# SyncE's and GpSimd's instructions in program order, with several loads moved, in a spectral-convolution and dilation kernel

## The chip, the core and the metric

The kernel runs on one core of a Trainium2 chip. TensorE (PE) multiplies matrices, VectorE (DVE) and ScalarE (ACT) work on tiles, GpSimd (POOL) and SyncE (SP) here do little but issue transfers (DMAs) between the main memory and the on-chip memory. Each engine works through its own instructions in order; engines wait for each other and for transfers through semaphores. The metric is the device time of one execution in microseconds (us). The kernel before takes 4047.03 us, the median of 3 runs (4043.34 to 4052.0).

## The reference

The input x has 8 images of 8 channels in 4 groups, 256 x 256 pixels each, in float32.

```python
def ref(x, ...):                           # cut to what matters
    # layer 0: x + FNO(groupnorm(x))
    h = gconv1x1(concat(x_normed, gridx, gridy), fc0)     # 2 + 2 -> 10 channels in each of 4 groups
    for i in range(4):
        h1 = irfft2(12 x 12 low modes of rfft2(h), lo and hi, times sp_w1[i], sp_w2[i])
        h2 = gconv1x1(h, w_w[i], w_b[i])
        h = h1 + h2
        if i < 3:
            h = x*sigmoid(x*softplus(beta))/1.1 of h
    h = the same swish of gconv1x1(h, fc1)                # 10 -> 128 channels per group
    x = x + gconv1x1(h, fc2)                              # 128 -> 2 channels per group
    # layer 1: x + 3x3 dilation (max over the window, border -2) of groupnorm(x)
    return x + dilate3x3(groupnorm(x))
```

## The kernel before

Each image goes through four spectral layers, in which its state h stays on the chip in 11 chunks of 128 x 2048 numbers; the last layer stores the chunks to main memory. The "head" (fc1, swish, fc2: 128 steps) of an image reads them back in pieces hs and runs interleaved with the four layers of the next image. The dilation of the image before that runs in between. Beside the last layer of an image, the spectrum of the next image's x is made (`start`). The Python code records the instructions; inside `manual_schedule` the engines listed keep the order of the code. In this kernel these are TensorE, VectorE and ScalarE; the order of SyncE and GpSimd is chosen by the scheduler.

```python
    def load_x(b):                                   # 2 transfers of 1 MB
        src = a["x"][b].rearrange("c (p i f) -> (c p) i f", p=16, i=2)
        for i in range(2):
            nc.sync.dma_start(turned[:, i], src[:, i])
    ...
    def spectrum_x(b, out_):
        x = turned[:, 0:2]
        if b > 0:
            load_x(b)
        yield 1.5 * SIDE
        ...                                          # batch-norm statistics, transposes, transforms
    def load_sw(l, k):                               # 400 KB of spectral weights, two buffers "sw"
        t = sb.tile([128, G, 2 * WID, WID], F32, tag="sw")
        nc.sync.dma_start(t.rearrange("p g m i -> p (g m i)"), a["spw"][l, k])
        return t

    def mix(b, l, out_):
        ...
        for k in range(3):
            for k2 in range(2):
                pr = turned[:, 2, 1024 * k2 : 1024 * k2 + 800].rearrange(...)
                nc.vector.tensor_tensor(pr, sw[k], bt[:, k2, k]..., ALU.mult)          # L360
                yield 0.7
                nc.vector.tensor_reduce(s[k2][:, k]..., pr..., AX.X, ALU.add)          # L363
                if k == 0 and k2 == 1:
                    sw.append(load_sw(l, 2))
                yield 0.7
        ...
        nc.vector.tensor_tensor(f[:, 0], ..., ALU.subtract)                            # L371
        nc.vector.tensor_tensor(f[:, 1], ..., ALU.add)
        ...                                          # p_f: matmuls of fold with f        L379
    def layer(b, l, out_, stored, side):
        ...
        def burst(c):
            pair = [ps_z(f"p_z_{b}_{l}_{c}_{i}") for i in range(2)]
            ...                                      # L477 (l = 0) or L480, then L483, into pair
            for i in range(2):
                dst = h[:, c, 2 * i : 2 * i + 2, :]
                if l < 3:
                    nc.scalar.activation(dst, pair[i], AF.Silu)                        # L489
                else:
                    nc.scalar.activation(dst, pair[i], AF.Identity, bias=bias3)        # L491
            if l == 3:
                nc.sync.dma_start(stored[c], h[:, c].rearrange("p f w -> p (f w)"))    # L493, 1 MB

        def read_x(c):                               # 4 transfers of 48 KB
            for g in range(G):
                nc.sync.dma_start(
                    h[32 * g : 32 * g + 6, c].rearrange("p f w -> p (f w)"), a["xp"][b, c, g])
        if l == 0:
            for c in range(NCH):
                read_x(c)
            ...
        if l == 3:
            room = 0.0
            yield "odd"
            for c in range(NCH):
                burst(c)
                room += SIDE
                while room > 0.0:
                    room -= next(side, SIDE)         # side: start() of the next image
                yield (LAST,)                        # two head steps
            return
        ...
    def start(b, out_):
        if b < n_img:
            out_["sw"] = [load_sw(0, 0), load_sw(0, 1)]
            yield from spectrum_x(b, out_)
            for n in mix(b, 0, out_):
                yield 1.4 * n
    ...
    def head(b, stored, stats):
        ...
        def load_state(k):                           # 256 KB, four buffers "hs"
            if k < NQ * NCH:
                j, c = k // NCH, k % NCH
                hs[k] = sb.tile([128, PIX], F32, tag="hs", bufs=4, name=f"hs_{b}_{k}")
                nc.sync.dma_start(hs[k], stored[c][:, PIX * j : PIX * (j + 1)])
        def first(n):
            ...                                      # 8 matmuls L628, 2 activations L630
        def second(n):
            ...                                      # at n % 16 == 0 also the load of y; matmuls L650
            ...                                      # add to y on VectorE, L653 or L655
        load_state(0)
        load_state(1)
        for n in range(STEPS):
            if n % 32 % NBLK == 0:
                load_state(n // 32 * NCH + n % 32 // NBLK + 2)
            if n % 2 == 0 and n > 3:
                second(n - 4)
            first(n)
            yield
        second(STEPS - 4)
        second(STEPS - 2)
```

Line numbers such as L360 are those of the kernel before.

## Time and profile before

| engine | busy us | share of 4041.6 us |
|---|---|---|
| TensorE matmuls | 3734.7 | 92% |
| ScalarE | 2853.1 | 71% |
| VectorE | 2538.8 | 63% |
| GpSimd | 117.0 | 3% |

The transfers move 345.05 MB, 85 GB/s on average. The profiled execution took 4041.6 us. The views show, in this order: the busy share of each engine, in 40 equal slices a digit for tenths of the slice (9 is 90% or more); groups of instructions as "line engine operation, what it writes <- what it reads, count | busy us, mean ns | idle us before them and what ended it"; waits as "engine line <- who ended it: total us, times, longest us"; and the timeline as "start us, duration us, engine, line, operation". SPq is SyncE's queue: its entries are the issuing of a transfer, not the transfer. PEld is the loading of weights into TensorE.

### The profile page before, as it was taken

What the parts mean: (1) busy time and instruction counts of PE and PEld (TensorE: products, weight loads), DVE (VectorE), ACT (ScalarE), POOL (GpSimd) and SP (SyncE); (2) the same over time, 40 slices, a digit from 0 to 9 for tenths busy, and PEclk for the clock granted to TensorE, in tenths of its full rate; (3) what the DMA queues carried; (4) which work ended last, traced back from release to release, by engine and by line L of the source; (5) the groups of instructions that cost most, each with busy time, mean ns of one, the idle gap of its engine ahead of it and who ended that gap; (6) DMA issues with size and microseconds to landing.
All of it is one profiled execution on the core that took longest, in us unless ns stands there. A gap on an engine that the chain in (4) does not pass through costs nothing.

```text
span 4041.6 us, 118640 instructions
## 1 busy us (share of the span) xinstructions
PE 3734.7 (92%) x53530; PEld 1463.3 (36%) x53530; DVE 2538.8 (63%) x3535; ACT 2853.1 (71%) x2991; POOL 117.0 (3%) x202
## 2 busy tenths in 40 slices
PE   5666999999999999999999999999999999999997
PEld 2333333433333333333433333333333333333221
DVE  6765656556766666766666666666676666673533
ACT  3334777777777777777777777777777777778886
POOL 1000000000000000000000000000000000000000
PEclk8888999999999999999999999999999999999998
DMA  3005111432125321252122611144121532215311
GB/s 85 14 14 188 53 33 41 139 123 58 58 67 166 93 59 58 82 189 56 55 64 89 197 44 53 53 134 151 55 59 51 164 109 63 61 48 194 96 53 46
DMA packets 113985, 345.05 MB, mean 85 GB/s; under 512 B 15768, under 2 KB 18392, under 8 KB 98056
## 3 DMA queue, kind: packets, MB, share of 16 engines
q1 hardware_dynamic: 95288, 276.33, 22.0%
q0 software_dynamic: 18192, 61.13, 4.7%
q8 instruction: 422, 6.91, 0.7%
q14 instruction: 83, 0.68, 0.1%
HBM read 213.40 MB, written 123.74 MB: 83 GB/s over the span
## 4 chain that ended last, share of the span: by engine, by line
PE 78%; DVE 11%; ACT 7%; issue 3%; DMA 1%; POOL 0%; DVEq 0%; POOLq 0%; SPq 0%; ACTq 0%
PE p_fc L650 22%; PE p_fc L628 20%; PE p_z L483 8%; PE p_z L480 7%; PE p_d L448 6%; ACT act L630 4%; PE p_u L462 3%; PE p_z L477 3%; DVE turned L431 2%; PE p_b L333 2%; PE p_g L405 2%; PE p_g L410 2%; ACT h L491 2%; DVE turned L324 2%; DVE turned L201 1%
## 5 line engine op out<-in xcount | busy, mean ns | idle before, releaser
L630 ACT ACTIVATE act<-p_fc 128x1024 f32<-128x1024 f32 x2048 | 1960.1, 1026 | 669.6 <-PE p_fc L628 665.3
L628 PE MATMUL p_fc<-hs,c_w 32*128 32x512 f32 x8192 | 1204.4, 631 | 14.8 <-DVE turned L195 8.5
L650 PE MATMUL p_fc<-act,c_w 128*32 128x512 f32 x8192 | 997.5, 601 | 47.1 <-ACT act L630 35.5
L628 PEld LDWEIGHTS p_fc<-hs,c_w 32*128 32x128 f32 x8192 | 402.3, 183 | 697.3 <-ACT act L630 278.5
L489 ACT ACTIVATE h<-p_z 128x1024 f32<-128x1024 f32 x528 | 511.7, 1021 | 190.5 <-PE p_z L483 189.8
L431 DVE STREAM_TRANSPOSE turned<-h 128x1024 f32<-128x1024 f32 x528 | 623.2, 1219 | 23.4 <-ACT h L489 23.1
L655 DVE TENSOR_TENSOR y<-p_fc,y 128x512 f32<-128x512 f32 x392 | 270.6, 690 | 497.1 <-PE p_fc L650 496.1
L650 PEld LDWEIGHTS p_fc<-act,c_w 128*32 128x32 f32 x8192 | 227.5, 109 | 645.6 <-issue 345.5
L483 PE MATMUL p_z<-c_binv,zt 32*128 32x256 f32 x5632 | 411.7, 405 | 0.6 <-ACT zt L193 0.6
L480 PE MATMUL p_z<-h,c_wt 32*32 32x512 f32 x8448 | 371.1, 601 | 6.7 <-DVE y L655 3.4
L483 PEld LDWEIGHTS p_z<-c_binv,zt 32*128 32x128 f32 x5632 | 261.6, 186 | 305.4 <-issue 295.8
L448 PE MATMUL p_d<-turned,c_fw 32*32 32x480 f32 (+1 forms) x9216 | 309.9, 540 | 11.1 <-DVE turned L431 11.1
L195 DVE COPY zt<-p_g 128x264 f32<-128x264 f32 x300 | 162.6, 629 | 167.1 <-PE p_g L410 91.6
L491 ACT ACTIVATE h<-p_z,c_bias 128x1024 f32<-128x1024 f32 x176 | 186.5, 1111 | 38.8 <-PE p_z L483 38.4
L199 ACT ACTIVATE turned<-p_d 128x960 f32<-128x960 f32 x144 | 130.1, 903 | 94.5 <-PE p_d L448 94.5
L363 DVE TENSOR_REDUCE S<-turned 128x80 f32<-128x800 f32 x192 | 188.8, 983 | 4.7
L448 PEld LDWEIGHTS p_d<-turned,c_fw 32*32 32x32 f32 x9216 | 121.5, 103 | 187.1 <-issue 150.6
L360 DVE TENSOR_TENSOR turned<-t,B 128x800 f32<-128x800 f32 x192 | 188.6, 982 | 0.9 <-DMA t<-in_spw 0.8
L462 PE MATMUL p_u<-turned,c_stack 128*32 128x480 f32 (+1 forms) x1152 | 137.3, 546 | 42.9 <-DVE turned L201 42.9
L324 DVE STREAM_TRANSPOSE turned<-zt 128x960 f32<-128x960 f32 x96 | 175.6, 1857 | 0.6
L201 DVE COPY turned<-p_d 128x960 f32<-128x960 f32 x144 | 152.1, 1057 | 28.9 <-PE p_d L448 28.7
L480 PEld LDWEIGHTS p_z<-h,c_wt 32*32 32x32 f32 x8448 | 93.7, 103 | 211.2 <-ACT act L630 69.1
(169 smaller groups left out, 1964.8 us busy)
## 6 DMA issues: line engine op xcount, KB each, us to landing
stored<-h SPq DMA_DIRECT2D x88, 1024.0 KB
hs<-stored SPq DMA_DIRECT2D x352, 256.0 KB
t<-in_spw SPq DMA_DIRECT2D x96, 400.0 KB
yin<-y_rows POOLq DMA_DIRECT2D x56, 512.0 KB, 5.0
h<-in_xp SPq DMA_DIRECT2D x352, 48.0 KB
turned<-in_x SPq DMA_DIRECT2D x16, 1024.0 KB
y<-in_x SPq DMA_DIRECT2D x56, 256.0 KB
y_rows<-y POOLq DMA_DIRECT2D x56, 256.0 KB, 2.3
```

Source lines behind the costliest of these rows:

```text
L324: nc.vector.transpose(rows[:, 960 * g : 960 * (g + 1)].rearrange("p (i r) -> p i r", r=32), windows(g))
L431: nc.vector.transpose(dst[:, 2 * i : 2 * i + 2], h[:, c, 2 * i : 2 * i + 2].rearrange("p f (s x) -> p f s x", s=2))
L448: mm(pair[q // 2][part(v % 4), q % 2, : 240 * n], fw8[part(q), v, :], t[part(q), :, :, v, : NBLK * WID], start=v < 4, stop=v >= 4)
L462: mm(p[part(g), : 240 * n], stack, m, start=True, stop=True)
L480: mm(o, wt[part(q), l, g, :], h[part(q), c, f, :], start=True, stop=False)
L483: mm(pair[q // 2][:, q % 2, HW * s : HW * (s + 1)], zt[part(q), 2 * c + s].rearrange("p f o -> p (f o)"), binv[part(q), :], start=False, s ...
L489: nc.scalar.activation(dst, pair[i], AF.Silu)
L491: nc.scalar.activation(dst, pair[i], AF.Identity, bias=bias3)
L628: mm(pair[g // 2][:, g % 2, :], w1[part(g), blk, :], hs[k][part(g), :], start=True, stop=True)
L630: nc.scalar.activation(act[:, 2 * i : 2 * i + 2, :], pair[i], AF.Silu)
L650: mm(acc[part(g), :], w2[:, g, 15 - rb - i : 47 - rb - i], act[:, g, :], start=i == 0, stop=i == 1)
L655: nc.vector.tensor_tensor(y, sums, y, ALU.add)
```

## The change

SyncE and GpSimd join the engines that keep the order of the code. Since the scheduler then no longer moves loads ahead, the code asks for some of them in other places: the next image's x in front of the last layer, the first layer's x at first for four chunks and then four chunks ahead of each burst, the first two pieces of the head's state in the last burst of the last layer, and each y of the head eight steps before the first use. The arithmetic and the instructions of TensorE, VectorE and ScalarE are unchanged.

```diff
+AHEAD = 4
...
     def spectrum_x(b, out_):
         x = turned[:, 0:2]
-        if b > 0:
-            load_x(b)
         yield 1.5 * SIDE
...
+    def read_x(b, c):
+        for g in range(G):
+            nc.sync.dma_start(
+                h[32 * g : 32 * g + 6, c].rearrange("p f w -> p (f w)"), a["xp"][b, c, g])
...
         def burst(c):
+            if l == 0 and c + AHEAD < NCH:
+                read_x(b, c + AHEAD)
+            if l == 3 and c == NCH - 1:
+                for k in range(2):
+                    out_["pieces"][1](k)
             pair = [ps_z(f"p_z_{b}_{l}_{c}_{i}") for i in range(2)]
...
         if l == 0:
-            for c in range(NCH):
-                read_x(c)
...
                 yield from mix(b, l, d)
+            if l == 3 and b + 1 < n_img:
+                load_x(b + 1)
+            if l == 0:
+                for c in range(AHEAD):
+                    read_x(b, c)
             yield from rows_of(b, l)
...
-    def head(b, stored, stats):
-        hs, acts, box = {}, {}, {}
+    def pieces_of(b, stored):
+        hs = {}
+        def load_state(k):
+            if k < NQ * NCH and k not in hs:
+                ...                                  # as before
+        return hs, load_state
+
+    def head(b, pieces, stats):
+        hs, load_state = pieces
+        acts, ys = {}, {}
...
+        def load_y(t):
+            ...
+            nc.sync.dma_start(y, a["x"][b]...[:, t])
...
-        load_state(0)
-        load_state(1)
+        load_y(0)
         for n in range(STEPS):
+            if n % 16 == 8 and n // 16 < 7:
+                load_y(n // 16 + 1)
...
-    with tc.manual_schedule(engines={PE, DVE, ACT}):
+    with tc.manual_schedule(engines={E.PE, E.DVE, E.Activation, E.SP, E.Pool}):
...
+            d["pieces"] = pieces_of(b, stored)
```

## The prediction

> **What bounds the kernel now.** I read the page's busy shares and 40 slices first, then the busy time by stretch of one image, then the waits of each engine, and last the timelines of SyncE, VectorE (DVE), ScalarE (ACT) and TensorE (PE) around the end of an image's last layer.

> Span, TensorE and its slices, from the page:

> ```profile
> span 4041.6 us, 118640 instructions
> PE 3734.7 (92%) x53530; PEld 1463.3 (36%) x53530; DVE 2538.8 (63%) x3535; ACT 2853.1 (71%) x2991; POOL 117.0 (3%) x202
> ...
> PE   5666999999999999999999999999999999999997
> ```

> TensorE is full except in the first four slices (image 0 alone, no head beside it) and the last (the last head alone). Two steady images, busy time by engine (PE, PEld, DVE, ACT, POOL, clock, DMA share, GB/s):

> ```profile
> 900.00:1380.00 480.00, 462.72 (x6670) 180.29 (x6656) 318.18 (x442) 352.69 (x368) 14.68 (x24) 1.00 0.29 91
> 1380.00:1860.00 480.00, 462.69 (x6658) 179.64 (x6650) 318.75 (x443) 350.60 (x366) 14.69 (x24) 0.99 0.29 91
> ```

> An image gives TensorE 17.3 us of idleness in 480, and the DMA engines are busy for only 0.29. TensorE's largest waits from 420 to 3760 us:

> ```profile
> PE p_u L462 <- DVE turned L201: 35.5, 45, 2.4
> PE p_fc L650 <- ACT act L630: 21.6, 75, 0.5
> PE p_fc L650 <- ACT h L491: 10.6, 47, 0.3
> PE p_b L333 <- DVE turned L324: 9.9, 14, 0.7
> ```

> No transfer is among them. On VectorE, transfers end 33 us of idleness in the whole run: the dilation's reads (22.2 and 4.6), two small loads at the start (3.6 and 2.0) and one spectral weight:

> ```profile
> L360 DVE TENSOR_TENSOR turned<-t,B 128x800 f32<-128x800 f32 x192 | 188.6, 982 | 0.9 <-DMA t<-in_spw 0.8
> ```

> So there is no wait for a transfer to win back in the steady part. I compared the instructions of the two programs: those of TensorE, VectorE and ScalarE stand in the same sequence; only SyncE's and GpSimd's queues differ. The question is therefore only whether something lands later than it is needed.

> [...] a 0.4 MB weight issued 0.4 us after a 1 MB store was usable 5.5 us later. [...] the page of this kernel shows one hardware queue, with 276 of the 345 MB. [...] the trace has them, 116 before the first layer's matmuls with a median of 51 ns.

> **The change, part by part.**

> (1) *Next image's x ahead of the last layer.* The before queue already had it there: it was issued at 726.44 us, and the batch-norm statistics that read it started at 771.27. Now it follows the mix of layer 3, some 741 to 745 us on that clock. Two MB, at the 338 to 416 GB/s that the busiest 5 us stretches of the trace show, take 6 us; it lands 18 us early at least. Effect: 0.

> (2) *First layer's x four chunks ahead.* The first 16 of 44 small reads now follow the last store; the rest come one chunk per burst. Before, 30 of them took 22.15 us from 372.18, or 0.74 us each. Sixteen take 12 us. In the first steady boundary the last store is issued at 848.09, so they would be out by 860; layer 0's first matmul is at 868.17 and needs only the first four. Each later chunk has four bursts' lead, above 20 us. Effect: 0.

> (3) *Head's loads.* hs_0 and hs_1 now go just before the last store (about 841 us), the first head matmul that needs them is at 860.43: 19 us for 256 KB. y_0 and hs_2 follow the 16 reads at about 861; the add that needs y_0 comes after 871, hs_2 is used from step 6, after 885. Later hs loads wait for a buffer freed about ten steps before use; a step is 480/128 = 3.75 us. In the last head y_0 waits for the edge fills, now after the store of y at 3739.77, so about 3741; it is needed at 3749.40. Effect: 0.

> (4) *Program order on SyncE.* Here is the loss. The third weight of the next image's first mix (t, k = 2) is asked for when the first product frees a buffer. Before, the scheduler let it pass ahead of store 9. In program order it stands behind store 9, which waits for ScalarE's copy of burst 9; hs_0 follows it. At all seven boundaries the new queue reads store 9, t, hs_0. SyncE before, at the first steady boundary:

> ```profile
> 831.91 0.35 SPq L350 DMA_DIRECT2D t<-in_spw  x1
> ...
> 833.51 0.35 SPq L493 DMA_DIRECT2D stored<-h  x1
> ...
> 841.27 0.35 SPq L493 DMA_DIRECT2D stored<-h  x1
> ```

> The copy that frees store 9, the products of k = 2 that need t, the sum after them, and TensorE's next step, each from its engine's timeline:

> ```profile
> 837.76 2.12 ACT L491 ACTIVATE h<-p_z,c_bias 128x1024 f32<-128x1024 f32 x2 [0.20 <-PE p_z L483]
> ...
> 841.53 0.98 DVE L360 TENSOR_TENSOR turned<-t,B 128x800 f32<-128x800 f32 x1
> ...
> 847.32 0.69 DVE L655 TENSOR_TENSOR y<-p_fc,y 128x512 f32<-128x512 f32 x1 [1.86 <-PE p_fc L650]
> 847.92 0.27 DVE L371 TENSOR_TENSOR F<-S,S 128x120 f32<-128x120 f32 x1
> ...
> 848.34 1.02 PE L379 MATMUL p_f<-F,c_fold 32*32 32x120 f32 x32
> ```

> How long t takes behind a store is seen at image 0's boundary, on SyncE and then VectorE:

> ```profile
> 367.15 0.35 SPq L493 DMA_DIRECT2D stored<-h  x1
> 367.59 0.38 SPq L350 DMA_DIRECT2D t<-in_spw  x1
> ...
> 373.12 0.99 DVE L360 TENSOR_TENSOR turned<-t,B 128x800 f32<-128x800 f32 x1 [0.83 <-DMA t<-in_spw]
> ```

> That is 373.1 - 367.15 = 5.95 us after the store's issue. Now the sum for the first steady boundary: the copy ends at 837.76 + 2.12 = 839.9, store 9 goes at 840.0 and t is usable at about 846.0 instead of being there at 841.5: VectorE stands 4.4 us. Its two products and two reductions take 4 x 0.98, to 849.9; the add of y pushes the sum F to 0.6 later, 850.5, and L379 starts 0.4 after F, at 850.9 in place of 848.34: 2.6 us. The difference to 4.4 is the 1.86 us that VectorE stood idle there already. The same working gives 2.5 us at the second boundary (copy ends about 1321.5, need 1323.39, L379 at 1329.96) and 2.0 at the third (copy ends 1802.9, need 1805.33, L379 at 1811.91); the other three look like the third (copy ends 2288.15, need 2290.57, L379 at 2297.15). At image 0's boundary store 9 was issued at 369.58, so t would come at 375.5 instead of 373.1 with TensorE already waiting: 2.4 us. Sum: 2.4 + 2.6 + 2.5 + 4 x 2.0 = 15.5 us. TensorE is in order and full, so most of it stays; ScalarE catches up during the stall and saves perhaps a few of the later short waits, so I book 13.

> (5) *Waits.* The new program has 49 more EventSemaphores on TensorE, 11 more on VectorE and 67 fewer on ScalarE. At 51 ns they would be +2.5, +0.6 and -3.4 us were they all exposed; most are behind running work. Booked: -1.

> (6) *GpSimd in program order.* Before, the edge fills of the last head blocked GpSimd for 33.6 us at 3646 to 3680 us; that is gone, but TensorE had no wait for the dilation there. In steady images one read of yin moves behind two stores of y, which are done before the last layer begins; its reader comes one burst into that layer. Effect: 0.

> Prediction: 4047 + 13 - 1 = 4059 us, 0.3% slower.

> **Rivals.** *No difference, or a small gain.* If t lands in 3 us rather than 5.5, VectorE's 1.86 us of slack hides nearly all of it, and the lighter ScalarE queue decides: 4040 to 4050. For it speaks that the small x reads no longer share the queue in that stretch; against it that the store in front is the same. *A blocked SyncE queue starves the head.* One queue in program order means any store or buffer wait holds up all behind it. If hs or x came too late each burst of layers 0 and 3 would wait: 1 us on 22 bursts in 7 images is 154 us, 4200. Against it stands the lead of 10 us or more for each of them in (2) and (3). *A faster steady part.* That would need idleness ended by transfers; TensorE has 17.3 us per image in all, 7 x 17.3 = 121 us, and none of its waits names one.

> **Range and chances.** The delay per boundary may be 0 to 3.5 us, over seven boundaries 0 to 25; the effects booked at zero add some 5 us either way. From 4047 that gives 4042 to 4077, which I move down a little for the lighter ScalarE queue: 4040 to 4076. Two per cent is 81 us: a gain of that size would take two thirds of the steady idleness and can't come from transfers, chance 0.01; a loss needs the starved head, 0.03; within 2%, 0.96.

> **What would show it.** In the changed profile VectorE's product with t (L360's group) should have idleness ended by the DMA t<-in_spw of some 20 to 30 us, in seven waits of 2 to 4.5 us, where there was one of 0.8. TensorE should have waits of about 2 us more than before at p_f on VectorE's F, once per boundary, and its busy time in a steady image should stay at 463 us while the image takes 482 to 484. No wait of TensorE should name hs or in_xp. It is wrong if t shows no wait, if TensorE waits for a transfer, or if the stretch up to 330 us moves by more than 2 us.

## The result, and the profile after

The changed kernel took 4086.03 us (median of 4 executions, 4080.85 to 4087.45) beside 4045.59 us for the kernel before. The ratio is 1.0095, with a 95% interval of 1.0078 to 1.0113. A second series gave 4080.59 beside 4049.87, ratio 1.0086 (1.0058 to 1.0114). The prediction was 4059 with a range to 4076: the direction was right, the size was less than half of what came.

The page of the kernel after, span, busy time and slices:

```profile
span 4083.4 us, 118516 instructions
PE 3757.7 (92%) x53530; PEld 1470.7 (36%) x53530; DVE 2538.0 (62%) x3535; ACT 2853.3 (70%) x2991; POOL 117.1 (3%) x202
PE   5666999999999999999999999999999999999997
```

TensorE, VectorE, ScalarE and GpSimd execute as many instructions as before. VectorE and ScalarE are as busy as before to within a microsecond, but TensorE's busy time grew from 3734.7 to 3757.7 us with the same 53530 matmuls. So this is not only a matter of waiting: the same matmuls lasted longer.

The predicted part is there. The product with the third weight t, in the groups of the page:

```profile
L359 DVE TENSOR_TENSOR turned<-t,B 128x800 f32<-128x800 f32 x192 | 188.4, 981 | 23.9 <-DMA t<-in_spw 23.8
```

That is 23.8 us of idleness where there was 0.8. TensorE's largest waits from 420 to 3760 us:

```profile
PE p_u L466 <- DVE turned L202: 35.5, 45, 2.4
PE p_fc L662 <- ACT act L651: 20.7, 74, 0.3
PE p_f L378 <- DVE F L370: 11.2, 6, 2.3
PE p_fc L662 <- ACT h L500: 9.9, 45, 0.3
```

The third line is new: six waits of TensorE for F, up to 2.3 us. No wait of TensorE names hs or in_xp. The other lines stand much as before.

The first steady boundary, on SyncE, ScalarE, VectorE and TensorE, each from its engine's timeline (start, length, what it is, and in brackets the idleness before it):

```profile
851.47 0.32 SPq L502 DMA_DIRECT2D stored<-h  x1
851.88 0.39 SPq L349 DMA_DIRECT2D t<-in_spw  x1
...
849.32 2.12 ACT L500 ACTIVATE h<-p_z,c_bias 128x1024 f32<-128x1024 f32 x2 [0.20 <-PE p_z L492]
...
857.36 0.99 DVE L359 TENSOR_TENSOR turned<-t,B 128x800 f32<-128x800 f32 x1 [4.19 <-DMA t<-in_spw]
...
861.81 0.27 DVE L370 TENSOR_TENSOR F<-S,S 128x120 f32<-128x120 f32 x1
...
862.23 1.82 PE L378 MATMUL p_f<-F,c_fold 32*32 32x120 f32 x32 [2.30 <-DVE F L370]
```

ScalarE's copy ends at 851.44, store 9 goes at 851.47, t behind it, and t is usable at 857.36: 5.89 us after the store, where 5.95 was reckoned. VectorE stands 4.19 us (4.4 reckoned) and TensorE 2.30 us (2.6 reckoned).

Two things in these traces were in no step of the prediction. The first is in the last line: the 32 matmuls of p_f take 1.82 us, and took 1.02 before. The busy time by stretch around them (PE, PEld, DVE, ACT, POOL, then the granted TensorE clock, DMA share and GB/s):

```profile
855.20:862.00 6.80, 4.54 (x44) 1.42 (x36) 4.57 (x7) 6.20 (x7) 0.00 (x0) 1.00 0.82 299
862.00:865.40 3.40, 3.17 (x42) 2.03 (x42) 1.50 (x8) 0.00 (x0) 0.00 (x0) 0.51 0.41 82
865.40:872.00 6.60, 6.60 (x48) 2.54 (x40) 3.22 (x6) 4.76 (x5) 0.00 (x0) 1.00 0.43 93
...
892.70:903.00 10.30, 10.30 (x78) 3.07 (x70) 2.90 (x5) 5.71 (x6) 0.00 (x0) 0.50 0.25 58
```

For 3.4 us from the end of the wait, and again for 10.3 us from 892.7, TensorE runs at half its clock (0.51 and 0.50 granted) while it is busy for 3.17 of the 3.40 us and for all of the 10.30. Between 386 and 3740 us the clock records of this trace hold 64.8 us of such stretches, each 3.41 us long or a multiple; the trace of before holds 27.3 us. By estimate, half of the 37.5 us more is lost, about 18.8 us, if TensorE is busy throughout.

The second is in layer 0's second burst of each image. TensorE's timeline there, the kernel before and then the kernel after, with ScalarE's of the kernel after below it:

```profile
874.09 1.18 PE L477 MATMUL p_z<-h,wcn 6*32 6x512 f32 x32
```

```profile
889.41 1.05 PE L486 MATMUL p_z<-h,wcn 6*32 6x512 f32 x4
890.65 1.14 PE L486 MATMUL p_z<-h,wcn 6*32 6x512 f32 x28 [0.19 <-ACT act L651]
...
889.58 1.94 ACT L651 ACTIVATE act<-p_fc 128x1024 f32<-128x1024 f32 x2 [1.05 <-PE p_fc L649]
```

Before, the 32 matmuls start together. After, four start and the others come 1.24 us later, when ScalarE has read the first half of a head tile: 889.58 plus half of 1.94 is 890.55. Most of that wait counts as busy: the four that run cover 1.05 of the 1.24 us, and 0.19 are idle. The instructions are the same. What they wait for is not, as the two programs say of the second PSUM tile of this burst:

```
before  L477 Matmult p_z, layer 0, chunk 1, second half <- h,wcn   waits: DMA, VectorE
after   L486 Matmult p_z, layer 0, chunk 1, second half <- h,wcn   waits: DMA, ScalarE
```

All tiles in PSUM, the memory into which TensorE writes, share four buffers, and the scheduler chooses one for each tile. With SyncE and GpSimd in program order it has chosen otherwise: 28 of the 4001 tiles follow another tile in their buffer than before. One of them at each of the seven boundaries is this one, which now takes a buffer that ScalarE frees late, while a head tile gets the one that VectorE had freed. By what rule the scheduler chooses is not shown.

### The profile page after: what moved, and what is told of

It reads as the page before. It is cut to its first block, busy times and chain, and to the rows that moved or that the text cites. A ratio compares the mean times of both kernels' runs of the same rounds, so it can differ in the third digit from the quotient of the medians.

```text
span 4083.4 us, 118516 instructions
## 1 busy us (share of the span) xinstructions
PE 3757.7 (92%) x53530; PEld 1470.7 (36%) x53530; DVE 2538.0 (62%) x3535; ACT 2853.3 (70%) x2991; POOL 117.1 (3%) x202
## 2 busy tenths in 40 slices
PE   5666999999999999999999999999999999999997
## 3 DMA queue, kind: packets, MB, share of 16 engines
q1 hardware_dynamic: 95288, 276.33, 22.2%
## 4 chain that ended last, share of the span: by engine, by line
PE 76%; DVE 12%; ACT 7%; issue 3%; DMA 2%; POOL 0%; SPq 0%; DVEq 0%; POOLq 0%; ACTq 0%
PE p_fc L662 22%; PE p_fc L649 20%; PE p_z L492 8%; PE p_z L489 7%; PE p_d L452 6%; ACT act L651 4%; PE p_u L466 3%; DVE turned L435 3%; PE p_z L486 2%; PE p_b L332 2%; PE p_g L409 2%; PE p_g L404 2%; DVE turned L323 2%; ACT h L500 2%; DVE turned L202 1%
## 5 line engine op out<-in xcount | busy, mean ns | idle before, releaser
L359 DVE TENSOR_TENSOR turned<-t,B 128x800 f32<-128x800 f32 x192 | 188.4, 981 | 23.9 <-DMA t<-in_spw 23.8
```

## The experiments

Times scatter from execution to execution, by 9 to 18 us where a series has 12 or more, and the mean granted clock scatters with them (0.974 to 0.979 in the 65 executions of the kernel before). The table therefore has, beside the medians and the ratio, the mean of span times clock (what the span would be at TensorE's full clock, if TensorE were busy throughout) and the mean of span times (1 - clock) (what the reduced clock took, on the same condition), each with its standard error. Much of the latter lies in the first 386 us: 66.6 us in the trace of before and 63.1 us in that of after, at a granted clock of 0.83 and 0.84. The condition fails for e7: in its trace TensorE stands idle for 44 of the 140 us at half clock from 386 to 3740 us, so its 165.4 says too much.

| kernel | executions | median us | ratio to before, 95% | span x clock | lost to the clock |
|---|---|---|---|---|---|
| before, beside e1 to e12 | 65 | 4047.93 to 4050.61 | 1 | 3951.9 +- 0.3 | 96.3 +- 0.6 |
| after | 4 | 4086.03 | 1.0095 (1.0078 to 1.0113) | 3975.1 +- 1.4 | 108.2 +- 2.7 |
| e5, after again | 4 | 4080.59 | 1.0086 (1.0058 to 1.0114) | 3977.4 +- 1.0 | 103.0 +- 4.0 |
| e1, t ahead of store 9 | 4 | 4066.16 | 1.0040 (1.0025 to 1.0055) | 3963.8 +- 1.8 | 100.6 +- 2.6 |
| e2, buffers of before | 4 | 4069.39 | 1.0051 (1.0036 to 1.0066) | 3967.2 +- 1.8 | 101.7 +- 2.9 |
| e3, both | 20 | 4055.53 | 1.0010 (1.0003 to 1.0018) | 3956.4 +- 0.6 | 96.9 +- 1.3 |
| e4, before with after's buffers | 7 | 4063.38 | 1.0026 (1.0014 to 1.0038) | 3960.5 +- 1.9 | 99.8 +- 3.3 |
| e6, after with dummies | 4 | 4083.84 | 1.0085 (1.0067 to 1.0103) | 3977.3 +- 1.1 | 103.0 +- 3.1 |
| e7, program order alone | 4 | 4217.26 | 1.0414 (1.0391 to 1.0436) | 4048.1 +- 2.8 | 165.4 +- 5.9 |
| e8, moved loads alone | 12 | 4047.64 | 0.9996 (0.9986 to 1.0006) | 3953.3 +- 1.1 | 93.1 +- 1.8 |
| e9, before, buffers named | 12 | 4048.47 | 0.9998 (0.9990 to 1.0007) | 3951.1 +- 0.9 | 96.1 +- 1.5 |
| e10, before, buffers by release | 4 | 4030.84 | 0.9957 (0.9942 to 0.9972) | 3942.7 +- 0.8 | 87.7 +- 2.0 |
| e11, moves, buffers by release | 5 | 4031.42 | 0.9956 (0.9942 to 0.9970) | 3944.1 +- 1.2 | 85.4 +- 2.7 |
| e12, order, t first, by release | 5 | 4032.18 | 0.9966 (0.9952 to 0.9980) | 3945.8 +- 1.2 | 86.3 +- 2.8 |

The theory after the result (A): the loss is t's stall, plus the swapped buffer, plus half clock that follows such waits. Rival B: the half clock falls where it falls, and only the waits themselves can be won back. Rival C: the small x reads in layer 0, and TensorE's additional waits for them (352 waits for transfers in its program, 229 before), cost most.

**e1, t ahead of store 9.** Store 9 is asked for one burst later; t then precedes it in the queue.

```diff
-            if l == 3:
-                nc.sync.dma_start(stored[c], h[:, c].rearrange("p f w -> p (f w)"))
+            for j in {9: (), 10: (9, 10)}.get(c, (c,)) if l == 3 else ():
+                nc.sync.dma_start(stored[j], h[:, j].rearrange("p f w -> p (f w)"))
```

> The kernel after, but store 9 is asked for one burst later, so that the third weight t goes ahead of it; everything else, the PSUM buffers too, as after. Three theories of the 40 us. A (waits, and the half clock that follows them): t's stall is 13.7 us of TensorE's waits at p_f, and part of the 18.8 us lost at half clock follows those waits; 4086 falls to 4060 to 4067, VectorE's idleness for t below 2 us, and the half-clock time falls from 64.8 us to 40 to 50 us. B (waits alone; the half clock falls where it falls): 4070 to 4074, half-clock time 55 to 75 us. C (the small x reads and TensorE's extra waits for them cost most): 4075 to 4086.

4066.16 us, within A. VectorE's wait for t, of which two short ones are left:

```profile
DVE turned L359 <- DMA t<-in_spw: 1.3, 2, 1.0
```

Span times clock fell by 12.4 us from the 3976.2 that the two series of the kernel after average, close to the 13.7 us by which TensorE's waits at p_f had grown (46.4 to 60.1 over the whole run). The half-clock time of the trace, 54.6 us, lies above the 40 to 50 that A expected and just under B's 55: the time favours A, this one trace does not.

**e2, the buffers of before.** Each tile is given by name the buffer that it had in the kernel before; the string has one digit per tile, in order of creation.

```diff
+    buffer = iter(BUFFER)
     def ps_z(name):
-        return ps.tile([128, 2, 512], F32, tag="z", bufs=4, name=name)
+        return ps.tile([128, 2, 512], F32, tag="z" + next(buffer), bufs=1, name=name)
...
+BUFFER = ("03210321032103210321031203120132..." [4001 digits])
```

> The kernel after, with each PSUM tile given by name the one of the four buffers that it had in the kernel before. In the kernel after, the second half of layer 0's second burst waits at every boundary for ScalarE's release of a head tile where it used a buffer freed by VectorE before. A: 7 x 1.2 = 8.4 us of direct wait goes, with a little of the half clock: 4070 to 4079. B: 4076 to 4079. C: no change, 4084 to 4088, the wait before the second burst is then the x reads'.

4069.39 us, just under A's range, and 9.0 us less in span times clock. TensorE's weight loads for layer 0 waiting for ScalarE's reading of the head, the kernel after and then e2:

```profile
PEld p_z L486 <- ACT act L651: 27.2, 49, 1.1
```

```profile
PEld p_z L486 <- ACT act L651: 19.2, 42, 0.8
```

Seven waits of 1.1 us are gone, 8.0 us in all, and 42 remain, as in the kernel before:

```profile
PEld p_z L477 <- ACT act L630: 19.4, 42, 0.8
```

By C the wait would have stayed, as the x reads are unchanged. C falls for this burst.

**e3, both edits.**

> Both edits: t ahead of store 9, and the PSUM buffers of before. A: all three terms are gone, 4043 to 4052, half-clock time near the 27.3 us of before. B: 4062 to 4066 with half-clock time unchanged at 55 to 75 us. C: above 4066.

4055.53 us. It missed A's 4043 to 4052 by 3.5 us, though B and C are further off. Span times clock is 4.5 us above that of before; the loss to the clock is back at its old value, 96.9 against 96.3. C falls here for layer 0 as a whole: TensorE's 352 waits for the x reads are all still in this program, yet layer 0's matmuls on x, matched one by one with those of before outside the half-clock stretches, are spaced as before, to 0.1 us in sum. The execution whose trace is kept was among the longer ones (span 4061.1, 58.0 us at half clock), so the mean over 20 says more about the clock than the trace.

**e4, the kernel before with after's buffers.** The same edit as in e2 on the kernel before, with the other string.

> The kernel before, with each PSUM tile given the buffer that it has in the kernel after; queues, loads and order as before. A and B: 8.4 us of direct wait at layer 0's second burst, and by A a few us of half clock behind it: 4054 to 4062. C: 4043 to 4048.

4063.38 us, 1.4 us above the range of A and B and far from C. Span times clock rose by 8.6 us without any transfer touched. In the trace most of the growth sits in layer 0's matmuls on x: matched in the same way, they lie some 7 us further apart in this run and in the kernel after. Removed from the kernel after (e2: 9.0; e3 against e1: 7.4) or added to the kernel before (8.6), the swap costs the same within the errors of about 2 us.

**e5, the kernel after again.** No edit.

> The kernel after once more, so that it stands on the same chip as the others and its half-clock time is known from several executions. All theories: 4082 to 4092. A: the span times its mean granted clock, which leaves the half clock out, is 20 to 25 us above that of before (3951.7 us over 26 executions in the first series), and the rest, 10 to 18 us, is half clock.

4080.59 us, as expected in time; span times clock 25.5 us above before, half a microsecond over the expectation, and the clock's loss 6.7 us above, below the 10 to 18 expected. With errors of 2.7 and 4.0 us the two series (108.2 and 103.0) can't be told apart; together they put the clock's share at 9.3 us, with an error of 2.5.

**e6, dummies in front of p_f.** Four matmuls of constants keep TensorE at work while VectorE waits for t.

```diff
         p = ps_a(f"p_f_{b}_{l}")
+        if l == 0 and b > 0:
+            for i in range(4):
+                mm(p[:, 256 * (i % 2) : 256 * (i % 2) + 256], ident, binv, start=True, stop=True)
```

> The kernel after with its own buffers given by name, and four matmuls of constants (about 1.5 us, written to p_f's buffer and overwritten) in front of p_f at each of the seven boundaries, so that TensorE works while VectorE waits for t; the stall itself stays. Giving the buffers by name moves TensorE's first matmuls and takes some 4 us off the start. A (the half clock follows the wait at p_f): half-clock loss falls by 5 to 8 us as in the run with t first, 4072 to 4078. B (the half clock falls where it falls): 4080 to 4085, nothing but the shorter start.

The wait is filled, and p_f runs at full speed:

```profile
860.01 1.99 PE L377 MATMUL p_f<-c_binv,ident 128*128 128x256 f32 x8
862.26 1.02 PE L381 MATMUL p_f<-F,c_fold 32*32 32x120 f32 x32 [0.26 <-DVE F L370]
```

No half-clock stretch lies within 12 us behind p_f at any of the six steady boundaries; there were three in the first trace of the kernel after and two in that of e5. Yet the time is the same, 4083.84, and so is the clock's loss, 103.0 +- 3.1. So the half clock right behind p_f seems to follow the wait there, as far as three traces can show it, but in the sum nothing was won that these executions can show. On the total, B was right and A was wrong.

**e7, program order alone.** The kernel before, with SyncE and GpSimd in program order and the loads where they were.

```diff
-    with tc.manual_schedule(engines={PE, DVE, ACT}):
+    with tc.manual_schedule(engines={PE, DVE, ACT, mybir.EngineType.SP, mybir.EngineType.Pool}):
```

> The kernel before with SyncE and GpSimd in program order and nothing else: no load is moved. A: t again stands behind store 9 and the scheduler again swaps the buffer of layer 0's second burst, so all of the loss is here, 4078 to 4092. C (the moved loads cost): 4045 to 4060.

4217.26 us: neither theory. Without the moved loads, program order costs 167 us (4217.26 beside 4049.87). VectorE's two largest waits for transfers and its wait for t in the whole run, and two of TensorE's waits from 420 to 3760 us, of which the first was not there before and the second took 3.4 us:

```profile
DVE y L653 <- DMA y<-in_x: 151.8, 13, 19.5
DVE bn_x L234 <- DMA turned<-in_x: 67.7, 9, 14.6
DVE turned L360 <- DMA t<-in_spw: 22.3, 7, 4.0
...
PE p_st_y L209 <- DVE mv_y L206: 36.2, 6, 7.0
PE p_z L480 <- DVE y L655: 32.9, 11, 6.1
```

The next image's x (turned), whose load nothing moves ahead in this run, comes late. All 44 small x reads of layer 0 and an hs load now stand ahead of the head's load of y; SyncE's timeline and VectorE's add:

```profile
884.81 27.66 SPq L497 DMA_DIRECT2D h<-in_xp  x44
913.06 0.35 SPq L620 DMA_DIRECT2D hs<-stored  x1
913.76 0.35 SPq L643 DMA_DIRECT2D y<-in_x  x1
...
918.97 0.75 DVE L653 SCALAR_TENSOR_TENSOR y<-p_fc,c_b,y 128x512 f32<-128x512 f32 x1 [17.29 <-DMA y<-in_x]
```

The reads take 27.66 us, y is asked for at 913.76, and VectorE stands for 17.29 us. The moved loads keep most of this loss away from the program order; what they do by themselves is e8's question.

**e8, the moved loads alone.** The kernel after, SyncE and GpSimd left to the scheduler.

> The kernel after with SyncE and GpSimd left to the scheduler: the moved loads without the program order. Its PSUM buffers are those of before. A: 4045 to 4054, as before. C: 4070 to 4090.

4047.64 us, no difference to before. Of VectorE's wait for t this is left:

```profile
DVE turned L359 <- DMA t<-in_spw: 0.4, 1, 0.4
```

The 32 matmuls of layer 0's second burst start together again at all seven boundaries. In e7, where no load was moved, both are there: 22.3 us of waiting for t, and at each of the seven boundaries four matmuls and then 28. So the stall and the swap both come with the program order. Against C this run says less than e3 does, because only 268 of the 352 waits for x reads are in its program (229 before).

**e9, e10, e11: what the choice of buffers is worth.** e9 is the control for naming them, e10 and e11 give each tile the buffer whose last reader ended first in the trace of before (608 tiles then follow another tile), in the kernel before and in that of e8. The edit is e2's with other strings.

> The kernel before with each PSUM tile given by name the buffer it has anyway: a control for what naming does by itself. In the runs with named buffers TensorE's first matmuls had moved and about 4 us had gone from the start. All theories: 4043 to 4049, the start about 4 us shorter, nothing else.

> The kernel before, queues and loads as they were, but each PSUM tile takes the one of the four buffers whose last reader ended first in the trace of before (608 of 4001 tiles then follow another tile than before). In that trace 175 tiles started within a fraction of a microsecond of their buffer's release while another buffer had been free longer; summed, 47 us at most. If the choice of buffers is a cost of this kernel and not only of the swap at layer 0, 4015 to 4035; if the waits just move to the next tile, 4040 to 4050.

> The same buffers by release, on the kernel with the moved loads and with SyncE and GpSimd left to the scheduler, which alone took 4047.6 us. Same numbers as the run before it: 4015 to 4035 or 4040 to 4050, and within 4 us of it, since the moves alone changed nothing.

Naming alone does nothing (0.9998). The 4 us that were to go from the start do not: TensorE's first matmul moves from 11.7 to 17.2 us, but its twentieth stands at 25.2 us, where it stood at 25.4. By release, the kernel before takes 4030.84 and that of e8 4031.42: 0.43% and 0.44% faster than before, and both faster than the kernels before and after. The weight loads of layer 0 waiting for ScalarE, in e10:

```profile
PEld p_z L477 <- ACT act L630: 14.8, 36, 0.8
```

It was 19.4 us in 42 waits in the kernel before. Of the 47 us counted as an upper bound, 9.2 us came in span times clock and 8.6 us in lost clock, 17.8 together.

**e12, program order with both losses mended and the better buffers.**

> The kernel after, SyncE and GpSimd in program order, with t ahead of store 9 and the buffers by release: both known losses of the change mended, and the choice of buffers improved as in the two runs before (4031). A: what then still differs from those two is only the 4 to 5 us that have stayed with the program order in every run (TensorE's stops at issue among them): 4033 to 4041. If the program order costs nothing of its own: 4027 to 4033.

4032.18 us, within the range for a program order that costs nothing of its own and under A's 4033 to 4041. The kernel after, with t ahead of store 9 and the buffers chosen by release, is faster than before by 0.34%. Span times clock is 2.4 us above the mean of e10 and e11, with an error of 1.4: the remainder that goes with the program order is small, and this run cannot tell 0 from 4.

## Why the prediction was right and wrong

**The working of steps (1), (2), (3) held.** No wait of TensorE names hs or in_xp; moved alone (e8) the loads changed nothing. The 16 small reads took 11.53 us where 12 were reckoned. The rival of a starved head was reckoned at 4200 and set aside because of the leads in (2) and (3); e7 shows that these leads matter: without the moved loads it is 4217. That 4200 and 4217 lie so close is luck. The 4200 came from TensorE waiting 1 us for hs or x in each burst; in e7 no burst waits for either, but VectorE waits 151.8 us for y and 67.7 us for the next image's x.

**Step (4) held in mechanism and size.** Seven waits for t, 23.8 us for VectorE where 20 to 30 were named, 4.19 at the boundary worked out as 4.4. One reading was off: the copy at the second boundary ended at 1320.96 us, not 1321.5, which makes its 2.5 us 2.0, beside 1.77 measured. Waits at p_f grew by 13.7 us, booked as 13; taking the stall away gave 12.4 us (e1) and 10.8 us (e2 against e3) of full-clock time, each with an error of about 2.

**What failed first is a sentence ahead of the steps**: that the three engines' instructions stand in the same sequence, only SyncE's and GpSimd's queues differ, and "the question is therefore only whether something lands later than it is needed". The same sequence is not the same program. The choice of PSUM buffers had changed, and could have been read in the waits of layer 0's matmuls before anything ran: step (5) counted the waits and put 51 ns on each, the median of the 116 EventSemaphores in front of layer 0's matmuls on x (L477) in the trace of before, but a count does not tell whom each waits for. It cost 7.4 to 9.0 us, for which the sum had no term.

**Step (5) booked -1 for the changed waits, and no such gain is seen.** With t and the buffers mended, 4.5 us of full-clock time remain in e3, with an error of 0.7. The moves alone (e8) make 1.4 of them, with an error of 1.1; the rest goes with the program order, and e12 leaves its size open. The traces put some 3 us on stops of TensorE that no releaser explains, from 386 to 3740 us, before and then after:

```profile
PE p_g L410 <- issue: 1.1, 3, 0.6
```

```profile
PE p_g L409 <- issue: 2.9, 2, 1.6
PE p_fc L662 <- issue: 1.4, 1, 1.4
```

That is 4.3 us against 1.1; e3 has 4.5. Three stops of over 1 us come at the same three matmuls in the kernel after, e2, e3 and e5, with a fourth in e1, and within six matmuls of these in e12; the kernel before stops for 0.19 us at the first of them and not at the other two. No kernel with SyncE left to the scheduler has a stop above 0.8 us. Why is not shown, nor that the added waits are the cause.

**The sum had no term for the clock.** The prediction held that TensorE's busy time in a steady image would stay at 463 us per 480. The 480 was the length of its stretch and not of an image, which took 483.0 us already. The busy time is lower in such a stretch (460.35 in the mean of two), but an image now takes 487.3 us (p_f at 862.2 and, five images later, at 3298.9), which makes 467.4 us of busy time an image against 465.6. The matmuls at half speed are part of it: over the two series of the kernel after the clock took 105.6 us, 9.3 more than before.

So, in mean spans: t's stall 12.4, the buffers 7.4 (e1 against e3), the rest 4.5, together 24.3 us, which is the whole growth of the full-clock time (3976.2 - 3951.9), as it must be for differences taken one after the other; the independent checks of the first two terms are 10.8 and 9.0. With 9.3 us of clock that is 33.6 us, of which the prediction had the first term. The first series lies 7 us above this sum and the second 3 us below.

**Step (6)**, GpSimd's order, was not run by itself. **What stays open** is what decides how many half-clock stretches a boundary gets. From 386 to 3740 us, 5 of 6 in the trace of before and 10 of 16 in that of after lie 18 to 40 us behind p_f, around layer 0's first bursts. The loss grows with the waits (96.3, 96.9, 99.8, 100.6, 101.7, 105.6 us for before, e3, e4, e1, e2, after), though neighbours in this row lie within their errors, and filling the longest wait did not lower it. That the added waits cause the 9.3 us is therefore argued, not shown.

## What to carry to other kernels

When a queue is put in program order, go through every load that stands behind something which waits, and ask where each can be asked for earlier; here the loads that were moved separate 4217 from 4086 us, and one weight behind one store is half of the full-clock time that was still lost. Compare not only the order of instructions but what each waits for: a scheduler that chooses buffers may choose others when a queue changes that seems to have nothing to do with them. And where TensorE is full, give a new wait a second term, for the half clock that may come with it; here that term was 9.3 us beside 24.3 us of full-clock time, and that the waits cause it is not shown.
